# Second biases of a mixture-of-experts layer: added to the routed rows from a fetched table of eight rows, in place of one bias product per output bank

## The chip, the cores and the metric

The kernel runs on one core of a Trainium2 chip. The core has TensorE (PE in the profile), VectorE (DVE), ScalarE (ACT), GpSimd (POOL) and SyncE (SP), each with its own instruction queue that is worked off in order, and 16 DMA engines that all queues share. The metric is the device time of one execution in microseconds, lower is better.

## The reference

Two layers follow each other on x (625 nodes by 1024, f32). The first is a graph layer over 20000 edges of two types. The second, which the change concerns, is a feed-forward layer with two shared experts and eight routed ones, of which each node takes its two best:

```python
sh = _gelu(jnp.einsum('td,sdh->sth', xf, sW1) + sb1[:, None, :])
shared = jnp.einsum('sth,shd->std', sh, sW2) + sb2[:, None, :]
shared = shared.mean(axis=0)
gates = xf @ rW + rb
topk_vals, topk_idx = jax.lax.top_k(gates, TOP_K)
topk_probs = jax.nn.softmax(topk_vals, axis=-1)
...
h = _gelu(jnp.einsum('td,edh->eth', xf, W1) + b1[:, None, :])
y = jnp.einsum('eth,ehd->etd', h, W2) + b2[:, None, :]
moe = jnp.einsum('te,etd->td', w, y)
return (shared + moe).reshape(B, L, D)
```

The second biases are b2 (8 x 1024) and sb2 (2 x 1024). A node's output holds the mean of the two rows of sb2, and the sum of two rows of b2, weighted with its two probabilities, which add up to one.

## The kernel before

The program is one long straight line for the one core. The source calls helpers, and a scheduler places each engine's instructions; within an engine they then run in the order in which they were placed. A call's place in the source therefore doesn't fix where its instructions stand in an engine's queue. `tc.issue_after` holds an instruction back behind another one.

The stages, with the times of the profiled execution:

- Front and counting, to about 100 us. Edges are counted per pair of nodes with one-hot matrices: VectorE builds the one-hots (`ohs`, `ohk`, L849 to L852) and TensorE multiplies them (L868). Between these, node tiles t = 0 to 4 of 125 nodes go through `stats(t)` (VectorE bn_stats L757 and L760, then ScalarE's `h`, L765), `to_columns` (eight TensorE transposes L795; half of the result is written to `nT` by ScalarE, L801, the other half by VectorE, L798), and `project` (L891: eight f32 products over k into one bank, which read both halves of `nT`). The table `at(c, f, ...)` says after which count column each is called; `at(EC - 1, ...)` is the end of the counting. Then come the aggregation (L909) and the activation.
- Output projection of the graph layer and the second layer norm (L952 to L966), 102 to 133 us. GpSimd writes the rows to DRAM as `h2d` and `x1d`.
- Gate, `route`, `slots` and the shared experts' first product (`shared_in`, L1137), 134 to 170 us. `slots` gives each (node, expert) pair a place in NJ = 11 tiles of 128 slots. Two one-hots, `oh` (place in the tile) and `oj` (which tile, times the node's number `tid`), are multiplied (p_tok, L1250), which gives each slot's node. From it come `tok` (row to fetch) and `row` (row to write).
- The routed experts' first product, 170 to 221 us: GpSimd fetches the rows of each tile (`xs`, L1332, an indirect DMA; pool `io` with three buffers), TensorE transposes them (p_x, L1340) and multiplies with W1 (p_h, L1359).
- The routed experts' second product (p_yj, L1417), 221 to 260 us. A tile fills two PSUM banks of 512 columns; they are copied to `ys` by VectorE (L1421, 15 copies) or ScalarE (L1423, 7 copies), and GpSimd writes the tile to DRAM (`yt`, L1425, an indirect DMA).
- The shared experts' second product (p_o, L1472), 260 to 296 us, in eleven banks. SP loads the routed rows of each node from `yt` (`gs`, L1436); VectorE adds them with their weights `wab`, and adds the banks (L1448). The result is stored.

The second biases take this way in the kernel before. At the start GpSimd copies sb2 and b2 into a DRAM tile `bd`, three times over (L625, L627). After `slots`, `bias_parts` loads it (`b2x`) and splits it in three bf16 parts (`b23`); `weights_T` splits the weights `w` (two ones for the shared experts, eight for the routed) likewise and transposes them on TensorE into `wT` (L1298). In the last stage each p_o bank ends with one product of the two:

```python
nc.tensor.matmul(p[:TP, :n], wT[:, own], b23[:, at], start=False, stop=True)   # L1474
```

GpSimd's queue at the start holds, in this order: constants, the loads of `cb`, `vec` and `rb_t`, sums for `join` (L619, L621) with the two `bd` copies among them, and the load of `rw_t`. Its DMAs share eight completion semaphores in turn, so that a DMA waits for the one eight before it. SP's queue holds the loads of x and the weights, the clearing of `yt`, and then the loads of `w1a`, `sw1` and `w2a`.

Of the kernel before, what the change touches and what calls it, by code (L numbers as in the profile page):

```python
# [8 lines left out]
F32 = mybir.dt.float32  # L9
F16 = mybir.dt.float16  # L10
BF16 = mybir.dt.bfloat16
I32 = mybir.dt.int32
# [440 lines left out]
def sparse_kernel(  # L453
# [166 lines left out]
    for i in (2, 3):  # L620
        nc.gpsimd.tensor_add(join, join, ident[:, QC * i : QC * (i + 1)])  # L621


    bd = dram.tile([3, NS + NE, D], F32, name="bd")
    nc.gpsimd.dma_start(bd[:, :NS, :], bass.AP(tensor=sb2.tensor, offset=sb2.offset,  # L625
                                               ap=[[0, 3], [D, NS], [1, D]]))
    nc.gpsimd.dma_start(bd[:, NS:, :], bass.AP(tensor=b2.tensor, offset=b2.offset,  # L627
                                               ap=[[0, 3], [D, NE], [1, D]]))
    b23 = const.tile([3 * QC, D], BF16, name="b23")

    def bias_parts():
        b2x = io.tile([3 * QC, D], F32, tag="io", name="b2x")
        nc.vector.memset(b2x, 0.0)
        for j in range(3):
            nc.gpsimd.dma_start(b2x[j * QC : j * QC + 3 * (NS + NE)], bd.rearrange("i e d -> (i e) d"))
        b2h = rt.tile([3 * QC, D], BF16, name="b2h")
        for j in range(3):
            with tc.issue_after(named.ins):
                nc.vector.tensor_copy(b2h, b2x)
            nc.scalar.copy(b23[j * QC : (j + 1) * QC], b2h[j * QC : (j + 1) * QC])  # L640
            if j < 2:
                nc.vector.tensor_sub(b2x, b2x, b2h)

    rw_t = const.tile([128, KD, QC], F32, name="rw_t")
    nc.vector.memset(rw_t[:, :, NE:], 0.0)
# [338 lines left out]
    def at(c, f, *args):  # L984
        after[c].append((f, args))
# [13 lines left out]

    at(50, clear)  # L1000
    at(30, transpose_vec)
    at(6, scales, 0, 2)
    at(18, scales, 2, 4)
    at(21, scales, 4, NT)
# [90 lines left out]


    w = const.tile([TP, NT, NS + NE], F32, name="w")
    wT = hid.tile([3 * QC, N], BF16, name="wT")
    sel = const.tile([TP, NT, NE], F16, name="sel")
    wide = [TP, NT, NE]  # L1100

    def route():
        full = [TP, NT, NE, NE]
        other = gates[:, :, None, :].to_broadcast(full)
        own = gates[:, :, :, None].to_broadcast(full)
        nc.vector.tensor_scalar(lower, lower, 0.0, None, op0=ALU.is_gt)
        above = rt.tile(full, F32, name="above")
        equal = rt.tile(full, F32, name="equal")
        nc.vector.tensor_tensor(above, other, own, op=ALU.is_gt)
        nc.vector.tensor_tensor(equal, other, own, op=ALU.is_equal)  # L1110
        nc.vector.tensor_mul(equal, equal, lower[:, None, :, :].to_broadcast(full))
        nc.vector.tensor_add(above, above, equal)
        cnt = const.tile(wide, F32, name="cnt")
        nc.vector.tensor_reduce(cnt, above, axis=AX.X, op=ALU.add)
        nc.vector.tensor_scalar(sel, cnt, 1.5, None, op0=ALU.is_lt)
        top = const.tile([TP, NT], F32, name="top")
        nc.vector.tensor_reduce(top, gates, axis=AX.X, op=ALU.max)
        ex = const.tile(wide, F32, name="ex")
        nc.vector.tensor_sub(ex, gates, top[:, :, None].to_broadcast(wide))
        nc.scalar.activation(ex, ex, AF.Exp)  # L1120
        nc.vector.tensor_mul(ex, ex, sel)
        tot = const.tile([TP, NT], F32, name="tot")
        nc.vector.tensor_reduce(tot, ex, axis=AX.X, op=ALU.add)
        inv = const.tile([TP, NT], F32, name="tot_inv")
        nc.vector.reciprocal(inv, tot)
        nc.vector.memset(w[:, :, :NS], 1.0)
        nc.vector.tensor_mul(w[:, :, NS:], ex, inv[:, :, None].to_broadcast(wide))


# [15 lines left out]
    wab = const.tile([TP, 2, NT], F32, name="wab")  # L1145
    tok = const.tile([128, NJ], I32, name="tok")
    row = const.tile([128, NJ], I32, name="row")
    ej = const.tile([1, nt + 4], I32, name="ej")

    def slots():  # L1150
# [63 lines left out]
        nc.vector.tensor_reduce(ab[:, 1], m[:, 1], axis=AX.X, op=ALU.max)  # L1214
        both_ = [TP, 2, NT, NE]
        nc.vector.tensor_tensor(m, m, ab[:, :, :, None].to_broadcast(both_), op=ALU.is_equal)
        nc.vector.tensor_mul(m, m, w[:, None, :, NS:].to_broadcast(both_))
        nc.vector.tensor_reduce(wab, m, axis=AX.X, op=ALU.add)
        nc.vector.tensor_scalar(ab[:, 0], ab[:, 0], 4096.0, None, op0=ALU.add)
# [17 lines left out]
        nc.vector.tensor_copy(pc[:, 1], col)  # L1237
        oh = rt.tile([TP, 2, NT, 128], F16, name="oh")
        oj = const.tile([TP, 2, NT, NJ], F16, name="oj")
        q = ps_mm("p_tok")  # L1240
        for a in range(2):
            nc.vector.tensor_tensor(oh[:, a], it[:, None, :].to_broadcast([TP, NT, 128]),
                                    pc[:, 0, a][:, :, None].to_broadcast([TP, NT, 128]), op=ALU.is_equal)
            nc.vector.tensor_tensor(oj[:, a], it[:, None, :NJ].to_broadcast([TP, NT, NJ]),
                                    pc[:, 1, a][:, :, None].to_broadcast([TP, NT, NJ]), op=ALU.is_equal)
            nc.vector.tensor_mul(oj[:, a], oj[:, a], tid[:, a, :, None].to_broadcast([TP, NT, NJ]))
        shared_in(0, 1)
        for a in range(2):
            for t in range(NT):
                nc.tensor.matmul(q[:, :NJ], oh[:, a, t], oj[:, a, t],  # L1250
                                 start=(a == 0 and t == 0), stop=(a == 1 and t == NT - 1))

        t = rt.tile([128, 2, NJ], F32, name="t")
        nc.vector.tensor_scalar(t[:, 0], q[:, :NJ], float(YB), float(YB), op0=ALU.is_ge, op1=ALU.mult)
        nc.vector.scalar_tensor_tensor(t[:, 1], q[:, :NJ], -1.0, t[:, 0], op0=ALU.add, op1=ALU.subtract)
        named = nc.vector.tensor_scalar(tok, t[:, 1], 0.0, float(N - 1), op0=ALU.max, op1=ALU.min)
        nc.vector.tensor_scalar(t[:, 0], q[:, :NJ], 0.5, 4.0 * YB, op0=ALU.is_lt, op1=ALU.mult)
        nc.vector.tensor_tensor(row, t[:, 0], q[:, :NJ], op=ALU.add)

        for at in (0, NH2):  # L1260
            k = kt[:, 0, at : at + NH2]
# [15 lines left out]
        nc.vector.tensor_scalar(ej, es[:, : nt + 4], float(NE - 1), None, op0=ALU.min)  # L1277
        nc.vector.tensor_copy(flagf[:, 1:2], over[:1, 3:4])
        nc.vector.tensor_tensor(flag, flagf[:, 0:1], flagf[:, 1:2], op=ALU.add)
        return named  # L1280

    def weights_T():
        nc.vector.tensor_scalar(w[:, :, NS:], w[:, :, NS:], float(NS), None, op0=ALU.mult)
        NW_ = NS + NE
        part = rt.tile([TP, NT, 3 * QC], F32, name="part")
        nc.vector.memset(part, 0.0)
        near = const.tile([TP, NT, NW_], BF16, name="near")
        for i in range(3):
            nc.vector.tensor_copy(near, w)
            for j in range(3):  # L1290
                at = j * QC + i * NW_
                nc.vector.tensor_copy(part[:, :, at : at + NW_], near)
            if i < 2:
                nc.vector.tensor_sub(w, w, near)
        for a, b in ((0, 3), (3, NT)):
            p = ps_mm(f"p_wT_{a}")
            for d in range(a, b):
                nc.tensor.transpose(p[: 3 * QC, (d - a) * TP : (d - a + 1) * TP], part[:, d, :],  # L1298
                                    ident[:TP, :TP])
            nc.vector.tensor_copy(wT[:, a * TP : b * TP], p[: 3 * QC, : (b - a) * TP])  # L1300

    gate()
    route()
    named = slots()
    weights_T()
    bias_parts()
    for t in range(HK):
        shared_in(1, t)
    sh_in.close()
# [94 lines left out]
    for j in ORDER:  # L1404
        for a, _, e in parts(j)[1:]:
            for k in range(HK):
                w2m[j, a, k] = gat.tile([128, D], F32, tag="y", name=f"w2m_{j}_{a}_{k}")
                nc.scalar.copy(w2m[j, a, k][:, None, :], w2a[:, bass.ds(e, 1), k, :])
    sent = []
    for n, j in enumerate(ORDER):  # L1410
        y = gat.tile([128, D], F32, tag="y", name=f"ys_{j}")
        for s in range(2):
            at = slice(s * 512, (s + 1) * 512)
            p = ps_acc(f"p_yj_{j}_{s}")
            for k in range(HK):
                for a, b, e in parts(j):
                    made = nc.tensor.matmul(p[a:b], hjT[:, j, k, a:b],  # L1417
                                     w2m[j, a, k][:, at] if a else w2a[:, bass.ds(e, 1), k, at],
                                     start=(k == 0), stop=(k == HK - 1))
            if s or n < 4:  # L1420
                nc.vector.tensor_copy(y[:, at], p)  # L1421
            else:
                nc.scalar.copy(y[:, at], p)  # L1423

        sent.append(nc.gpsimd.indirect_dma_start(  # L1425
            out=yt, out_offset=bass.IndirectOffsetOnAxis(ap=row[:, j : j + 1], axis=0), in_=y, in_offset=None,
            bounds_check=2 * YB - 1, oob_is_err=False))
        for s in sent[:-1]:
            tc.declare_no_dep(sent[-1].ins, s.ins, reason="rows of different slots")

    gs = {}
    for d in range(NT):
# [26 lines left out]
    for d in range(NT):  # L1459
# [4 lines left out]
        for at in ((0, 512), (512, D)) if d < NT - 1 else ((0, 512), (512, 768), (768, D)):  # L1464
# [4 lines left out]
            with tc.issue_after(made.ins):  # L1469
                for i in range(NS):  # L1470
                    for k in range(HK):
                        nc.tensor.matmul(p[:TP, :n], shT[:, i, k, own], sw2[:, i, k, at],  # L1472
                                         start=(i == 0 and k == 0), stop=False)
                nc.tensor.matmul(p[:TP, :n], wT[:, own], b23[:, at], start=False, stop=True)  # L1474
            add(x1[:, d, at], p[:TP, :n], 1.0 / NS, x1[:, d, at])
            if d == NT - 1:
                store(d, at)
# [45 lines left out]
```

## Time and profile before

| | |
|---|---|
| time, median of three runs | 304.47 us (304.38 to 305.63) |
| profiled execution, time | 303.7 us |
| profiled execution, span | 301.4 us |
| PE busy | 290.8 us (96%) |
| VectorE busy | 168.4 us (56%) |
| ScalarE busy | 107.5 us (36%) |
| GpSimd busy | 45.2 us (15%) |
| DMA, mean over the span | 203 GB/s |

The span runs from the first to the last instruction; the profiled execution's own time is 2.3 us more. The page shows each engine's busy share in 40 slices of 7.5 us, the chain of waits that ended last, the groups of instructions by line, and the DMA issues. The timeline gives an engine's instructions in order: start and length in us, and in brackets how long the engine sat idle before one and what ended that.

### The profile page before, as it was taken

How to read it: one execution, taken by the hardware profiler on the slowest of the kernel's cores; microseconds unless marked ns; L12 is line 12 of the kernel's file. 1: busy time of each engine (PE TensorE's matmuls, PEld its weight loads, DVE VectorE, ACT ScalarE, POOL GpSimd, SP SyncE). 2: the span in 40 equal slices, each digit the busy share in tenths (PEclk: the TensorE clock that was granted, in tenths of full speed). 3: DMA queues.
4: the chain of work that ended last, by engine and by line, in shares of the span. 5: the costliest groups of instructions: out<-in, count | busy, mean ns of one | idle time of the engine just before them, and what ended most of it. 6: DMA issues, size and time to landing. Idle time of an engine off the chain costs nothing.

```text
span 301.4 us, 4682 instructions
## 1 busy us (share of the span) xinstructions
PE 290.8 (96%) x1649; PEld 194.9 (65%) x1649; DVE 168.4 (56%) x465; ACT 107.5 (36%) x246; POOL 45.2 (15%) x98
## 2 busy tenths in 40 slices
PE   8799999999999799999999999999999999999993
PEld 6687777787889534376777887887843334444452
DVE  5999999998327668756883122212223211255921
ACT  2455118355334432155123244638359311000000
POOL 9500000000000014240131212210003222200000
PEclk9999999999999999999999999999999999999998
DMA  7999910000009999965999253340057555479442
GB/s 243 304 318 393 421 65 2 0 2 1 0 17 340 348 348 391 400 195 182 348 396 410 86 203 96 114 141 3 0 190 276 221 209 210 191 291 385 161 138 73
DMA packets 27408, 61.15 MB, mean 203 GB/s; under 512 B 2176, under 2 KB 16007, under 8 KB 27375
## 3 DMA queue, kind: packets, MB, share of 16 engines
q1 hardware_dynamic: 21806, 43.77, 40.7%
q0 software_dynamic: 5280, 16.69, 15.7%
q10 hardware_dynamic: 294, 0.35, 0.5%
q8 instruction: 15, 0.25, 0.3%
q14 instruction: 13, 0.10, 0.1%
HBM read 42.76 MB, written 18.81 MB: 204 GB/s over the span
## 4 chain that ended last, share of the span: by engine, by line
PE 93%; DVE 4%; ACT 1%; issue 0%; ACTq 0%
PE p_pr L891 20%; PE p_h L1359 13%; PE p_yj L1417 13%; PE p_o L1472 11%; PE p_sh L1137 10%; PE p_y L952 6%; PE p_agg L909 6%; PE p_x L1340 3%; PE p_t L795 3%; PE cnt L868 2%; PE p_y L956 2%; PE p_hT L1371 1%; PE scrap L972 1%; PE p_gate L1085 1%; PE p_o L1474 1%; DVE ln_4s L727 0%
## 5 line engine op out<-in xcount | busy, mean ns | idle before, releaser
L891 PE MATMUL p_pr<-wg,nT 128*125 128x286 f32 x240 | 62.5, 409 | 0.0
L891 PEld LDWEIGHTS p_pr<-wg,nT 128*125 128x125 f32 x240 | 43.2, 187 | 11.3 <-ACT nT L801 0.2
L1359 PE MATMUL p_h<-w1a,xsT 128*128 (+2 forms) x176 | 40.0, 380 | 0.0
L1417 PE MATMUL p_yj<-w2a,hjT 128*128 (+2 forms) x88 | 38.6, 594 | 0.0
L1472 PE MATMUL p_o<-sw,shT 128*125 128x512 f32 (+1 forms) x88 | 36.1, 553 | 0.0
L1137 PE MATMUL p_sh<-h2T,sw 128*128 128x313 f32 (+1 forms) x128 | 35.2, 428 | 0.0
L1359 PEld LDWEIGHTS p_h<-w1a,xsT 128*128 128x128 f32 (+2 forms) x176 | 28.7, 168 | 7.4 <-issue 0.5
L1137 PEld LDWEIGHTS p_sh<-h2T,sw 128*128 128x128 f32 x128 | 23.6, 189 | 8.6 <-issue 0.2
L1417 PEld LDWEIGHTS p_yj<-w2a,hjT 128*128 128x128 f32 (+2 forms) x88 | 14.4, 168 | 22.4 <-issue 22.4
L1472 PEld LDWEIGHTS p_o<-sw,shT 128*125 128x125 f32 x88 | 16.4, 187 | 16.9 <-issue 16.2
L1421 DVE COPY ys<-p_yj 128x512 f32<-128x512 f32 x15 | 10.4, 692 | 28.7 <-PE p_yj L1417 26.5
L1363 DVE COPY hj<-p_h 128x256 f32<-128x256 f32 x11 | 4.7, 425 | 30.8 <-PE p_h L1359 30.8
L909 PE MATMUL p_agg<-P,CT 125*125 125x287 bf16 x150 | 20.1, 287 | 1.6 <-DVE agg L915 1.6
L966 POOL DMA_DIRECT2D x1d<-xh x10 | 5.3, 532 | 98.5 <-DVE xh L959 98.5
L909 PEld LDWEIGHTS <-CT 125*125 125x125 bf16 x150 | 18.5, 136 | 2.5 <-issue 2.0
L1425 POOL DMA_INDIRECT yt<-ys,row x11 | 10.8, 984 | 50.5 <-DVE ys L1421 50.5
L952 PE MATMUL p_y<-wo_t,eT 128*125 128x512 f32 x40 | 18.1, 595 | 0.0
L1332 POOL DMA_INDIRECT xs<-h2d,tok x11 | 11.2, 1015 | 45.0 <-PE p_x L1340 30.9
L1374 ACT ACTIVATE hjT<-p_hT,vT 128x128 f32<-128x128 f32 (+2 forms) x34 | 8.7, 332 | 24.5 <-PE p_hT L1371 24.5
L1344 DVE COPY xsT<-p_x 128x512 f32<-128x512 f32 x11 | 7.6, 692 | 17.4 <-PE p_x L1340 13.8
L1448 DVE SCALAR_TENSOR_TENSOR x<-p_o,x 125x512 f32<-125x512 f32 (+1 forms) x11 | 6.9, 641 | 16.3 <-PE p_o L1474 16.3
L1359 PE MATMUL p_h<-w1m,xsT 128*64 128x256 f32 (+1 forms) x96 | 14.7, 381 | 0.0
(302 smaller groups left out, 424.0 us busy)
## 6 DMA issues: line engine op xcount, KB each, us to landing
w1a<-in_L_ffn_W_dram SPq DMA_DIRECT2D x8, 1024.0 KB, 10.5
w2a<-in_L_ffn_W_dram SPq DMA_DIRECT2D x8, 1024.0 KB, 4.8
yt<-zero SPq DMA_DIRECT2D x2, 2560.0 KB
g<-yt SPq DMA_DIRECT2D x10, 512.0 KB, 6.7
sw<-in_L_ffn_sW_dram SPq DMA_DIRECT2D x4, 1024.0 KB, 5.0
x<-x1d SPq DMA_DIRECT2D x5, 500.0 KB
wg<-in_L_gnn_W_rel_dram SPq DMA_DIRECT2D x2, 1144.0 KB, 19.1
x1d<-xh POOLq DMA_DIRECT2D x5, 448.0 KB, 6.7
```

The costliest lines, as they stand in the source:

```text
L795: nc.tensor.transpose(pv[:, k, :], row[:, at : at + 128], ident[:TP, :TP])
L891: nc.tensor.matmul(p[:TP, :F], nT[:, k, m * TP : (m + 1) * TP], wg[:, k, r, :], start=(k == 0), stop=(k == KD - 1))
L909: nc.tensor.matmul(p[:TP, : F + 1], CT[:, m, at : at + TP], P[:, m, r, i], start=(m == 0 and i == 0), stop=(m == NT - 1 and i == 2))
L952: nc.tensor.matmul(ps[s][:TP, :], eT[:, k, :], wo_t[:, k, s * 512 : (s + 1) * 512], start=(k == 0), stop=False)
L1137: nc.tensor.matmul(p[:, : z - a], sw1[:, i, k, t * 128 : (t + 1) * 128], h2T[:, k, a:z], start=(k == 0), stop=(k == KD - 1))
L1332: nc.gpsimd.indirect_dma_start(out=xs, out_offset=None, in_=h2d, in_offset=bass.IndirectOffsetOnAxis(ap=tok[:, j : j + 1], axis=0))
L1340: nc.tensor.transpose(p[:, k * 128 : (k + 1) * 128], xs[:, at : at + 128], ident)
L1359: nc.tensor.matmul(p[a:b, :H], xsT[j][:, k, a:b], w1m[j, a][:, 0, k, :] if a else w1a[:, bass.ds(e, 1), k, :], start=(k == 0), stop=(k == ...
L1417: made = nc.tensor.matmul(p[a:b], hjT[:, j, k, a:b], w2m[j, a, k][:, at] if a else w2a[:, bass.ds(e, 1), k, at], start=(k == 0), stop=(k = ...
L1421: nc.vector.tensor_copy(y[:, at], p)
L1425: sent.append(nc.gpsimd.indirect_dma_start(out=yt, out_offset=bass.IndirectOffsetOnAxis(ap=row[:, j : j + 1], axis=0), in_=y, in_offset=No ...
L1472: nc.tensor.matmul(p[:TP, :n], shT[:, i, k, own], sw2[:, i, k, at], start=(i == 0 and k == 0), stop=False)
```

## The change

The biases of the routed rows are added where a tile's PSUM banks are copied out, from a table of eight rows in DRAM (`b2d`). Row e holds b2[e] plus half of each row of sb2; as a node's two weights add up to one, the mean of sb2 comes in whole through its two routed rows. The table is made at the start: three GpSimd DMAs load sb2[0] and sb2[1] (each repeated for the eight experts) and b2 into `b2p` (128 partitions, 64 columns each), `bias_rows` adds them with two VectorE instructions, and SP stores the sum. `slots` gets a second product (p_slot), of `oh` with `oe` (the tile's one-hot times the expert's number), which gives each slot's expert, `es_`. `fetch_bias(j)` fetches a row of the table for each of the tile's 128 slots with an indirect DMA from GpSimd, into the pool `io`; three are issued ahead of the p_yj loop, and one behind each `yt` write after that. The copies to `ys` become VectorE additions, all 22 of them. `bd`, `b2x`, `b23`, `bias_parts`, `weights_T`, `wT` and the eleven bias products go.

```diff
-    bd = dram.tile([3, NS + NE, D], F32, name="bd")
-    nc.gpsimd.dma_start(bd[:, :NS, :], bass.AP(tensor=sb2.tensor, offset=sb2.offset,
-                                               ap=[[0, 3], [D, NS], [1, D]]))
-    nc.gpsimd.dma_start(bd[:, NS:, :], bass.AP(tensor=b2.tensor, offset=b2.offset,
-                                               ap=[[0, 3], [D, NE], [1, D]]))
-    b23 = const.tile([3 * QC, D], BF16, name="b23")
-
-    def bias_parts():
-        b2x = io.tile([3 * QC, D], F32, tag="io", name="b2x")
-        nc.vector.memset(b2x, 0.0)
-        for j in range(3):
-            nc.gpsimd.dma_start(b2x[j * QC : j * QC + 3 * (NS + NE)], bd.rearrange("i e d -> (i e) d"))
-        b2h = rt.tile([3 * QC, D], BF16, name="b2h")
-        for j in range(3):
-            with tc.issue_after(named.ins):
-                nc.vector.tensor_copy(b2h, b2x)
-            nc.scalar.copy(b23[j * QC : (j + 1) * QC], b2h[j * QC : (j + 1) * QC])
-            if j < 2:
-                nc.vector.tensor_sub(b2x, b2x, b2h)
+    b2d = dram.tile([NE, D], F32, name="b2d")
+    BC = 128 // NE
+    b2p = fbig.tile([128, NS + 1, D // BC], F32, name="b2p")
+    for i, v in enumerate((sb2[0], sb2[1], b2)):
+        of = v.offset
+        ap = [[D // BC, 128], [1, D // BC]] if i == NS else [[0, NE], [D // BC, BC], [1, D // BC]]
+        nc.gpsimd.dma_start(b2p[:, i], bass.AP(tensor=v.tensor, offset=of, ap=ap))
+
+    def bias_rows():
+        for i in range(NS):
+            nc.vector.scalar_tensor_tensor(b2p[:, NS], b2p[:, i], 1.0 / NS, b2p[:, NS], op0=ALU.mult, op1=ALU.add)
+        nc.sync.dma_start(b2d.rearrange("e (c w) -> (e c) w", c=BC), b2p[:, NS])
...
+    at(EC - 1, bias_rows)
...
+        expert = const.tile([TP, 2, NT], F16, name="expert")
+        me = const.tile([TP, 2, NT, NE], F16, name="me")
+        nc.vector.tensor_tensor(me.rearrange("p a t e -> p (a t) e"), m.rearrange("p a t e -> p (a t) e"),
+                                it[:, None, :NE].to_broadcast([TP, 2 * NT, NE]), op=ALU.mult)
...
+        with nc.allow_low_precision("whole numbers up to 7"):
+            nc.vector.tensor_reduce(expert, me, axis=AX.X, op=ALU.add)
...
+            nc.vector.tensor_mul(oe[:, a], oj[:, a], expert[:, a, :, None].to_broadcast([TP, NT, NJ]))
             nc.vector.tensor_mul(oj[:, a], oj[:, a], tid[:, a, :, None].to_broadcast([TP, NT, NJ]))
...
+        q2 = ps_mm("p_slot")
+        for a in range(2):
+            for t in range(NT):
+                nc.tensor.matmul(q2[:, :NJ], oh[:, a, t], oe[:, a, t],
+                                 start=(a == 0 and t == 0), stop=(a == 1 and t == NT - 1))
...
+        nc.vector.tensor_scalar(es_, q2[:, :NJ], float(NE - 1), None, op0=ALU.min)
...
-    def weights_T():
-        nc.vector.tensor_scalar(w[:, :, NS:], w[:, :, NS:], float(NS), None, op0=ALU.mult)
...
-        for i in range(3):
-            nc.vector.tensor_copy(near, w)
-            for j in range(3):
-                at = j * QC + i * NW_
-                nc.vector.tensor_copy(part[:, :, at : at + NW_], near)
-            if i < 2:
-                nc.vector.tensor_sub(w, w, near)
-        for a, b in ((0, 3), (3, NT)):
-            p = ps_mm(f"p_wT_{a}")
-            for d in range(a, b):
-                nc.tensor.transpose(p[: 3 * QC, (d - a) * TP : (d - a + 1) * TP], part[:, d, :],
-                                    ident[:TP, :TP])
-            nc.vector.tensor_copy(wT[:, a * TP : b * TP], p[: 3 * QC, : (b - a) * TP])
...
-    sent = []
+    sent, biases = [], {}
+
+    def fetch_bias(j):
+        biases[j] = io.tile([128, D], F32, tag="io", name=f"b2_{j}")
+        nc.gpsimd.indirect_dma_start(out=biases[j], out_offset=None, in_=b2d,
+                                     in_offset=bass.IndirectOffsetOnAxis(ap=es_[:, j : j + 1], axis=0))
+
+    for j in ORDER[:3]:
+        fetch_bias(j)
...
-            if s or n < 4:
-                nc.vector.tensor_copy(y[:, at], p)
-            else:
-                nc.scalar.copy(y[:, at], p)
+            nc.vector.tensor_tensor(y[:, at], p, biases[j][:, at], op=ALU.add)
...
+        if n + 3 < NJ:
+            fetch_bias(ORDER[n + 3])
...
                         nc.tensor.matmul(p[:TP, :n], shT[:, i, k, own], sw2[:, i, k, at],
-                                         start=(i == 0 and k == 0), stop=False)
-                nc.tensor.matmul(p[:TP, :n], wT[:, own], b23[:, at], start=False, stop=True)
+                                         start=(i == 0 and k == 0), stop=(i == NS - 1 and k == HK - 1))
```

More of the change, by code (lines that the diff above doesn't have):

```diff
@@ L1097, in sparse_kernel @@
     w = const.tile([TP, NT, NS + NE], F32, name="w")
-    wT = hid.tile([3 * QC, N], BF16, name="wT")
     sel = const.tile([TP, NT, NE], F16, name="sel")
@@ L1125, in route @@
         nc.vector.reciprocal(inv, tot)
-        nc.vector.memset(w[:, :, :NS], 1.0)
         nc.vector.tensor_mul(w[:, :, NS:], ex, inv[:, :, None].to_broadcast(wide))
@@ L1147, in sparse_kernel @@
     row = const.tile([128, NJ], I32, name="row")
+    es_ = const.tile([128, NJ], I32, name="es_")
     ej = const.tile([1, nt + 4], I32, name="ej")
@@ L1239, in slots @@
         oj = const.tile([TP, 2, NT, NJ], F16, name="oj")
+        oe = const.tile([TP, 2, NT, NJ], F16, name="oe")
+        with nc.allow_low_precision("whole numbers up to 7"):
+            nc.vector.tensor_reduce(expert, me, axis=AX.X, op=ALU.add)
         q = ps_mm("p_tok")
@@ L1255, in slots @@
         nc.vector.scalar_tensor_tensor(t[:, 1], q[:, :NJ], -1.0, t[:, 0], op0=ALU.add, op1=ALU.subtract)
-        named = nc.vector.tensor_scalar(tok, t[:, 1], 0.0, float(N - 1), op0=ALU.max, op1=ALU.min)
+        nc.vector.tensor_scalar(tok, t[:, 1], 0.0, float(N - 1), op0=ALU.max, op1=ALU.min)
         nc.vector.tensor_scalar(t[:, 0], q[:, :NJ], 0.5, 4.0 * YB, op0=ALU.is_lt, op1=ALU.mult)
         nc.vector.tensor_tensor(row, t[:, 0], q[:, :NJ], op=ALU.add)
+        nc.vector.tensor_scalar(es_, q2[:, :NJ], float(NE - 1), None, op0=ALU.min)
         for at in (0, NH2):
@@ L1279, in slots @@
         nc.vector.tensor_tensor(flag, flagf[:, 0:1], flagf[:, 1:2], op=ALU.add)
-        return named
-    def weights_T():
-        nc.vector.tensor_scalar(w[:, :, NS:], w[:, :, NS:], float(NS), None, op0=ALU.mult)
[L1284 to L1287, printed above, removed]
-        for i in range(3):
-            nc.vector.tensor_copy(near, w)
-            for j in range(3):
-                at = j * QC + i * NW_
-                nc.vector.tensor_copy(part[:, :, at : at + NW_], near)
-            if i < 2:
-                nc.vector.tensor_sub(w, w, near)
-        for a, b in ((0, 3), (3, NT)):
-            p = ps_mm(f"p_wT_{a}")
-            for d in range(a, b):
-                nc.tensor.transpose(p[: 3 * QC, (d - a) * TP : (d - a + 1) * TP], part[:, d, :],
-                                    ident[:TP, :TP])
-            nc.vector.tensor_copy(wT[:, a * TP : b * TP], p[: 3 * QC, : (b - a) * TP])
     gate()
     route()
-    named = slots()
-    weights_T()
-    bias_parts()
+    slots()
     for t in range(HK):
```

## The prediction

> **What bounds the kernel now.** I read first the busy tenths of the page, then the chain that ended last in order of time, then the engine timelines around the places the change touches.
>
> ```profile
> PE   8799999999999799999999999999999999999993
> ...
> DVE  5999999998327668756883122212223211255921
> ...
> DMA  7999910000009999965999253340057555479442
> ...
> PE 93%; DVE 4%; ACT 1%; issue 0%; ACTq 0%
> ```
>
> Each digit covers 7.5 us. TensorE (PE) is full from the third slice to the last but one, and the chain is 93% PE. So every PE instruction added or removed counts at its full length, and whatever makes PE wait counts too. In slices 1 to 8 VectorE (DVE) is as full as PE: there it has no time in hand either. The DMA engines are full in slices 1 to 4, when x and the weights come in.
>
> The chain in the front stage (start, length, what):
>
> ```profile
> 10.30 0.29 PE cnt L868 x4
> 10.62 1.07 PE p_t L795 x8
> 11.70 0.11 PE cnt L868 x4
> 11.81 4.10 PE p_pr L891 x16
> 15.91 0.06 PE cnt L868 x2
> ```
>
> These are the first count matmuls, the transposes of node tile 0, and its first projection: eight f32 products over k (16 records, since each has two), of which the last four (from 11.81 + 2.05 = 13.86) read the half of nT that VectorE writes in to_columns. VectorE's timeline at that place (start, length, instruction, idle before it):
>
> ```profile
> 10.69 0.47 DVE L850 TENSOR_TENSOR ohs<-ohs,cols 125x512 f16<-125x512 f16 x1
> 11.74 0.68 DVE L798 TENSOR_TENSOR nT<-p_t,lT 128x500 f32<-128x500 f32 x1 [0.57 <-PE p_t L795]
> 12.33 1.28 DVE L757 BATCH_NORM_STATS2 st<-xh 125x6 f32<-125x512 f32 x2
> ```
>
> VectorE is free at 10.69 + 0.47 = 11.16; the eviction ends at 12.42, 1.44 before PE needs it. GpSimd's (POOL's) timeline shows when it issues the bias rows:
>
> ```profile
> 10.51 0.55 POOL L625 DMA_DIRECT2D bd<-in_L_ffn_sb_dram  x1 [2.34 <-DMA cb<-in_L_gnn_conv_bias_dram]
> 11.08 0.27 POOL L621 TENSOR_TENSOR join<-join,ident 128x32 f32<-128x32 f32 x1
> 11.28 0.53 POOL L627 DMA_DIRECT2D bd<-in_L_ffn_b_dram  x1
> 11.82 0.26 POOL L621 TENSOR_TENSOR join<-join,ident 128x32 f32<-128x32 f32 x1
> 12.02 0.96 POOL L646 DMA_DIRECT2D rw_t<-in_L_ffn_rW_dram  x1
> ```
>
> and the DMA list how long such transfers take from issue to landing (last column):
>
> ```profile
> bd<-in_L_ffn_b_dram POOLq DMA_DIRECT2D x1, 96.0 KB, 7.3
> ...
> rw_t<-in_L_ffn_rW_dram POOLq DMA_DIRECT2D x1, 32.0 KB, 7.7
> ...
> bd<-in_L_ffn_sb_dram POOLq DMA_DIRECT2D x1, 24.0 KB, 7.9
> ```
>
> Nobody on the path waits for bd before 143 us, so today these landings cost nothing.
>
> **What the Trainium skill says.** "DMA: Bandwidth & Descriptors", section "Anatomy of one DMA — SWDGE (gpsimd) path", prices a GpSimd DMA at about 2.0 us plus bytes over 436e3 per us; for 32 KB that would be an estimated 2.1 us. The trace disagrees: 6.1 to 7.9 us in this stretch, where the DMA engines are full. I use the trace. "TensorE: Matmul & The Clock Gate", section "Part 1: The HAM clock gate", says that after an idle window of about 3.4 us TensorE runs at half clock until it has been busy about as long. The trace agrees on the warming: the first 24 scrap matmuls take 2.74 us (114 ns each), the later 40 take 2.41 us (60 ns each). It has no idle gap long enough to show the cooling; the longest there is 1.69 us. "Perfetto Trace Analysis", section "Per-engine timelines", puts the wait for a semaphore in a queue ahead of execution; GpSimd shows the effect here: its join sum at 11.08 needs no DMA, yet stands behind the 2.34 us wait for cb.
>
> **The change part by part.**
>
> 1. *Bias products gone.* In the chain the eleven products at L1474 are nine of 0.22 and two of 0.11 and 0.13: 2.2 us off PE in the last stage, all on the path.
>
> 2. *weights_T and bias_parts gone.* The five transposes L1298 stand in the chain with 0.54 us: off. Their VectorE work (memset, three casts, two subtractions of 96x1024) and three ScalarE copies of 1.04 us lie beside p_sh, with PE busy throughout: nothing. GpSimd is freed of the 4.3 us it waited behind them; its gathers start earlier, but PE takes up the first p_x at 170.21 without a gap today: nothing.
>
> 3. *Expert per slot.* Ten p_slot matmuls like the ten of p_tok (0.24 us): +0.24. Four small VectorE instructions (me, its reduction, two oe) come ahead of the last oj, in steps of about 0.12 us: 0.5. The last oj ends at 152.28, PE arrives at 152.49, so PE waits about 0.3. Together +0.5 (bounds 0.2 to 0.8).
>
> 4. *The table.* b2p is filled by three GpSimd DMAs where bd had two, and bias_rows folds the shared biases in with two VectorE instructions of 128x64. The source calls bias_rows at the end of the counting, but the order of instructions as the changed kernel is built puts the two at rows 34 and 35 of VectorE, straight behind the ohs product that ends at 11.16 and ahead of the nT eviction; the first waits for the first and third b2p DMA. GpSimd's order: the first b2p still waits for cb (10.51), the second takes 11.28, the third stands where rw_t was, 12.02 to 12.5 (128 rows may take 0.8 to issue, as cb's 125 did). With 7.5 us to landing, between bd's and rw_t's: 12.1 + 7.5 = 19.6. VectorE stands from 11.16 to 19.6; two instructions of some 0.2 us follow; the eviction starts at 20.0 in place of 11.74: **VectorE is 8.3 us late**. Behind it in its queue are the statistics of tile 1, the one-hots of the next groups, and so everything PE gets. PE stops at 13.86 and resumes at 20.7: 6.8 late. It then catches nothing up, and loses more in two ways: half clock for about the 2.7 to 4.7 us that warming took at the start (from PE's first work at 1.5 or 2.5 to 5.2 or 6.2), costing half of that, 1.4 to 2.3; or, without it, ScalarE's h of tile 3, which follows VectorE's neg at 22.30 and ends at 23.72 for a p_t at 23.81, so that VectorE's 8.3 come through less 0.1. These overlap, they don't add: 8.2 on one path, 6.8 + 1.9 = 8.7 on the other. I take **8.6**. Later nothing absorbs it, as PE has no idle time until 96 us and little after. Bounds: landing after 6.1 (the shortest of this stretch) takes 1.5 off; 8 us and a slow issue add 1.
>
> 5. *b2d's store.* One 32 KB DMA on SP, between the two yt clears and the w1a loads. It waits for VectorE's two instructions, long done by then, and the w1a loads behind it wait for work up to 88 us: nothing.
>
> 6. *The gathers.* Eleven indirect DMAs on GpSimd, by the nearest row (xs: 0.94 to 1.4 us to issue, 4.4 to landing), three ahead, then one behind each scatter. GpSimd idles 2.4 us or more before each scatter, so 0.94 fits. The first three need io buffers freed by the last p_x groups (204 to 214), well before 222. A later gather is issued about 2 us after a tile ends and used 8.6 us after: 4.4 fits. They add 5.8 MB to the 40 us of p_yj; the DMA share there is 0.61, and 5.8 MB at about 385 GB/s (the 235 GB/s of that stretch over its 0.61) is 15 us of 39, or 0.38. That fills the engines but for bursts. I take nothing, bounds 0 to 4.
>
> 7. *The adds.* 22 VectorE additions from PSUM in place of 15 copies there and 7 on ScalarE: like L959 (125x512, 0.67 against the copy's 0.69), 15 us in a stage of 38: nothing.
>
> Sum: -2.2 - 0.5 + 0.5 + 8.6 = **+6.4**. The profiled execution had a span of 301.4 and took 303.7 us, 0.8 under the median 304.47; so 310.1 for such an execution, and 310.9 against the median.
>
> **The rivals.**
>
> *No stall: faster.* The place is the same two instructions; the price is only the landing. If it came by 11.5 us nothing would wait and -2.2 us would be left: 302.3. VectorE's lateness breaks even at 2.3 us, a landing at about 13.6, or 1.5 us after issue; above that the kernel is slower. Against it stand all landings of GpSimd's DMAs in this stretch, 6.1 or more. For it, only that SBUF rows of 256 bytes land sooner than bd did in DRAM; rw_t went to SBUF and took 7.7. Chance 0.06, with 0.02 for a landing that just balances.
>
> *A shorter stall.* Landing 4.4 after issue, as xs later: VectorE 5.2 late, PE 5.1, net +3: 307.5. Chance 0.07.
>
> *The gathers collide with the scatters.* All rows of a tile are mostly the same 4 KB of DRAM, and gathers share GpSimd's queue with the scatters. If scatters end so late that the g loads slip by more than 4 us past 268, PE and the last adds wait: another 4, 315. Against it: cb is one row read 125 times and landed in 6.7, like rows read once. Chance 0.07.
>
> **How the numbers follow.** The forecast has 0.78, at 310.9; its bounds (landing, clock, step 3) give 308.0 to 312.8. Adding the shorter stall's near edge, I give 307.8 to 312.8, which leaves out the no-stall and collision rivals. Half a per cent, 1.5 us, is about what a measurement can tell from no change. Faster 0.06, same 0.02, slower 0.92.
>
> **What would show it.** In the changed profile: the b2p instructions on VectorE with about 8 us of idle before them on a DMA; PE idle about 7 us in slice 1 or 2, then p_pr products longer for some 4 us; all later stages late by about 8.6, the p_o stage 2.2 shorter; y additions with no wait on a bias. A b2p wait under 3 us proves step 4 wrong; p_yj with gaps, or g loads that end later against p_o, prove step 6 wrong.

## The result, and the profile after

The changed kernel takes 318.13 us (median of six runs, 316.82 to 319.91), the kernel before 305.08 us in the same session. The ratio is 1.0436, with a 95% interval of 1.0407 to 1.0465: slower by 4.4%. The forecast was slower, 310.9 us, with a range of 307.8 to 312.8. The direction came out; the forecast added 6.4 us to the median of 304.47 that it started from, about half of the 13 us measured, and the time lies above the range.

The profiled execution has a span of 315.8 us, 14.4 more than before. Its page shows two holes in PE's row, one in slices 2 and 3 and one in slices 33 to 35 (a slice is 7.9 us here; the row PEclk is the granted TensorE clock, in tenths of full speed):

```profile
PE   8629999999999899999999999999999986799993
...
PEclk9969999999999999999999999999999999999999
```

The first hole is the forecast one. GpSimd's timeline, then VectorE's, then PE's, at the place shown for the kernel before:

```profile
10.72 0.67 POOL L630 DMA_DIRECT2D b2p<-in_L_ffn_sb_dram  x1 [2.58 <-DMA cb<-in_L_gnn_conv_bias_dram]
...
12.44 0.62 POOL L630 DMA_DIRECT2D b2p<-in_L_ffn_b_dram  x1
```

```profile
10.69 0.42 DVE L843 TENSOR_TENSOR ohs<-ohs,cols 125x512 f16<-125x512 f16 x1
20.48 0.48 DVE L634 SCALAR_TENSOR_TENSOR b2p<-b2p 128x64 f32<-128x64 f32 x2 [9.38 <-DMA b2p<-in_L_ffn_b_dram]
20.88 0.67 DVE L791 TENSOR_TENSOR nT<-p_t,lT 128x500 f32<-128x500 f32 x1
```

```profile
11.79 2.19 PE L884 MATMUL p_pr<-wg,nT 128*125 128x286 f32 x8
21.61 3.79 PE L884 MATMUL p_pr<-wg,nT 128*125 128x286 f32 x8 [7.63 <-DVE nT L791]
```

VectorE stands idle for 9.4 us, until the last b2p transfer has landed; the nT eviction comes at 20.88 in place of 11.74, and PE is idle for 7.6 us. The next eight records take 3.79 us, where the eight before the stall took 2.19: the granted clock was half of full speed from 18.05 to 24.9 us, and the clock row has its 6 there.

The second hole was not forecast. The groups that waited most (engine, line, what it waited for: us, times, longest), and the DMA list with the median to landing last:

```profile
DVE ys L1412 <- DMA b<-b2d,es__1591: 24.2, 7, 5.2
...
PE p_yj L1409 <- DVE ys L1412: 5.8, 4, 1.7
```

```profile
b<-b2d,es__1591 POOLq DMA_INDIRECT x11, 12.1
yt<-ys,row POOLq DMA_INDIRECT x11, 10.7
```

The bias rows land 12.1 us after their issue in the median (the profile gives a landing for six of the eleven gathers: the first took 4.5 us, the others 7.4 to 13.8). VectorE waits for them, the PSUM banks stay full meanwhile, and PE waits for banks. VectorE's timeline shows the pace that results, one tile about every 5.2 us where PE alone needs 3.4 (the step between the tiles before the first of these waits):

```profile
247.22 1.29 DVE L1412 TENSOR_TENSOR ys<-p_yj,b 128x512 f32<-128x512 f32 x2 [5.19 <-DMA b<-b2d,es__1591]
252.37 1.29 DVE L1412 TENSOR_TENSOR ys<-p_yj,b 128x512 f32<-128x512 f32 x2 [3.86 <-DMA b<-b2d,es__1591]
257.60 1.29 DVE L1412 TENSOR_TENSOR ys<-p_yj,b 128x512 f32<-128x512 f32 x2 [3.94 <-DMA b<-b2d,es__1591]
```

The balance follows from the starts of PE's groups in the two traces. At the last run of p_agg before the activation PE is late by 9.5 us (98.10 against 88.62), at the first p_x by 9.6 (179.62 against 170.04), at the first p_yj still by 9.6 (230.6 against 221.0), at the first p_o by 16.4 (275.9 against 259.5), at the end of the last addition by 14.2 (310.89 against 296.68). So the front cost 9.5, `slots` and the first products 0.1, **the second-product stage (first p_yj to first p_o) 6.8** (45.3 us against 38.5), and the p_o stage gave 2.2 back.

### The profile page after: what moved, and what is told of

Same layout as the page of the kernel before. It is cut to its first block, busy times and chain, and to the rows that moved or that the text cites. A ratio compares the mean times of both kernels' runs of the same rounds, so it can differ in the third digit from the quotient of the medians.

```text
span 315.8 us, 4651 instructions
## 1 busy us (share of the span) xinstructions
PE 292.1 (92%) x1643; PEld 194.8 (62%) x1643; DVE 165.4 (52%) x454; ACT 100.2 (32%) x236; POOL 54.6 (17%) x107
## 4 chain that ended last, share of the span: by engine, by line
PE 51%; issue 22%; DMA 11%; POOL 8%; DVE 6%; ACT 0%; POOLq 0%; DVEq 0%; ACTq 0%
PE p_pr L884 19%; PE p_o L1463 11%; PE p_y L945 5%; PE p_agg L902 5%; DMA b<-b2d,es__1591 4%; DMA xs<-h2d,tok 3%; DMA b2p<-in_L_ffn_b_dram 3%; POOL b L1397 2%; POOL xs L1316 2%; DMA cb<-in_L_gnn_conv_bias_dram 2%; PE p_t L788 2%; POOL yt L1414 2%; PE p_sh L1129 2%; PE p_y L949 2%; PE cnt L861 2%
## 5 line engine op out<-in xcount | busy, mean ns | idle before, releaser
L884 PE MATMUL p_pr<-wg,nT 128*125 128x286 f32 x240 | 64.3, 418 | 7.6 <-DVE nT L791 7.6
L884 PEld LDWEIGHTS p_pr<-wg,nT 128*125 128x125 f32 x240 | 44.2, 191 | 19.9 <-DVE nT L791 8.1
L1409 PE MATMUL p_yj<-w2a,hjT 128*128 (+2 forms) x88 | 39.7, 599 | 5.8 <-DVE ys L1412 5.8
L1463 PE MATMUL p_o<-sw,shT 128*125 128x512 f32 (+1 forms) x88 | 34.5, 553 | 0.0
L1412 DVE TENSOR_TENSOR ys<-p_yj,b 128x512 f32<-128x512 f32 x22 | 14.5, 688 | 35.0 <-DMA b<-b2d,es__1591 24.2
L1316 POOL DMA_INDIRECT xs<-h2d,tok x11 | 10.4, 950 | 55.3 <-PE p_x L1324 34.9
L1439 DVE SCALAR_TENSOR_TENSOR x<-g,wab,x 125x1024 f32<-125x1024 f32 x10 | 12.6, 1283 | 4.7 <-DMA g<-yt 4.5
```

What stands on the lines that cost most here:

```text
L884: nc.tensor.matmul(p[:TP, :F], nT[:, k, m * TP : (m + 1) * TP], wg[:, k, r, :], start=(k == 0), stop=(k == KD - 1))
L1316: nc.gpsimd.indirect_dma_start(out=xs, out_offset=None, in_=h2d, in_offset=bass.IndirectOffsetOnAxis(ap=tok[:, j : j + 1], axis=0))
L1409: made = nc.tensor.matmul(p[a:b], hjT[:, j, k, a:b], w2m[j, a, k][:, at] if a else w2a[:, bass.ds(e, 1), k, at], start=(k == 0), stop=(k = ...
L1412: nc.vector.tensor_tensor(y[:, at], p, biases[j][:, at], op=ALU.add)
L1439: added.append(nc.vector.scalar_tensor_tensor(*args, op0=ALU.mult, op1=ALU.add))
```

## The experiments

The first hole was put down to one wait, and that had to be tested. For the second hole there were three theories. A: the loads of x1, which SP issues at the start of the stage, occupy five of the 16 DMA engines, and the gathers and scatters have to pass through these five as well as the others. B: all 128 descriptors of a tile read the same one or few 4 KB rows of the table, and that is slow. C: GpSimd's queue cannot carry a gather behind every scatter.

A comes from what the Trainium skill says in "DMA: Bandwidth & Descriptors", section "Why a DMA increments its semaphore by 16 and not by 1": a transfer is spread over the largest number of engines, at most 16, that divides the outermost dimension of both its sides. An x1 load has 125 rows, so five. The DMA rows of the changed kernel, 40 slices of 245 to 270 us, agree:

```profile
DMA  9999633369889833496799333984977336578963
GB/s 380 374 380 334 210 144 131 131 249 380 282 282 367 302 118 131 184 406 243 216 419 295 131 125 131 367 341 184 380 282 288 144 125 262 203 197 347 328 203 118
```

Again and again the share falls to three tenths at about 131 GB/s. Five of 16 engines are 0.31, and 131 over five is 26 GB/s each, as much as each has when all are busy (420 over 16).

**late_rows**: the table's two VectorE instructions are held behind the last one-hot (`hot` collects the `ohk` instructions).

```diff
+    hot = []
+
     def bias_rows():
         for i in range(NS):
+          with tc.issue_after(hot[-1].ins):
             nc.vector.scalar_tensor_tensor(b2p[:, NS], b2p[:, i], 1.0 / NS, b2p[:, NS], op0=ALU.mult, op1=ALU.add)
...
-            nc.vector.tensor_tensor(halves(oh_k[:, :g, :]), row[:, None, :SPAN].to_broadcast(shape), key,
-                                    op=ALU.is_equal)
+            hot.append(nc.vector.tensor_tensor(halves(oh_k[:, :g, :]), row[:, None, :SPAN].to_broadcast(shape), key,
+                                               op=ALU.is_equal))
```

> The changed kernel, with the two bias_rows instructions held behind VectorE's last one-hot; nothing else changes. If the early wait for b2p costs what the profile of the changed kernel shows at the front (PE 9.5 us later at 98 us than before), 318.1 - 9.5 = 308.6 us, the second-product stage still 44 us long. If the front delay is taken up somewhere later, less than 5 us come back.

Measured: 309.87 us, ratio 1.016 (1.0125 to 1.0195), 8.3 us less than the changed kernel, 1.2 short of what was expected. In its chain the group of p_agg is back at its old start, and p_o starts late all the same:

```profile
88.62 7.47 PE p_agg L905 x60
...
266.27 34.37 PE p_o L1466 x88
```

The second-product stage runs from 221.1 to 266.1, 45.0 us. So the whole front delay seen in the profile came from that one wait, nothing took it up later, and the second hole stands by itself.

**x1_wide**: each x1 load in two parts, of 112 rows, which 16 divides, and 13 (`PARTS` are rows 0 to 111 and 112 to 124).

```diff
-        nc.sync.dma_start(x1[:, t, :], x1d[t * TP : (t + 1) * TP, :])
+        for g in PARTS:
+            nc.sync.dma_start(x1[g, t, :], x1d[t * TP + g.start : t * TP + g.stop, :])
```

> The changed kernel, with each x1 load of 125 rows issued as two (112 and 13 rows); nothing else changes. Theory A (five of the 16 DMA engines carry the x1 loads and are shared with gathers and scatters; they set the pace of 5.2 us a tile): the second-product stage falls from 44 to about 37.5 us, gathers land in about 5 us, 318.1 - 7 = 311 us. Theory B (a tile's 128 descriptors read one 4 KB row of DRAM, and that is slow) and theory C (GpSimd's queue is too slow for a gather behind each scatter): no change, 318.

Measured: 311.88 us, ratio 1.0241 (1.0196 to 1.0286), 6.3 us less. The stage runs from 231.1 to 270.7, 39.6 us. The DMA rows in 40 slices of 245 to 266 us no longer fall to three tenths:

```profile
DMA  9999999999999999999999889739899994967667
GB/s 273 281 289 273 281 304 304 359 421 445 382 281 242 289 343 429 429 398 437 414 406 445 359 336 421 312 133 343 242 250 297 414 336 187 304 195 203 242 258 320
```

GpSimd's queue moved 5.83 MB in these 21 us (278 GB/s), against 4.64 MB in 25 us (186 GB/s) of the changed kernel. The same gathers read the same rows through the same queue, so B and C cannot be what held them. The stage is still 1.1 us longer than the 38.5 before, and 2 us longer than expected: the engines are now full (a mean share of 0.94 over the stage), and while the x1 loads run one gather still takes 13.5 us, for which PE waits 0.9 us:

```profile
240.66 13.51 DMA b<-b2d,es__1591
```

**rows_apart**: as many gathers of the same size, but from rows that differ. The rows added are then not the biases, so that this run is for its time alone.

```diff
-        nc.gpsimd.indirect_dma_start(out=biases[j], out_offset=None, in_=b2d,
-                                     in_offset=bass.IndirectOffsetOnAxis(ap=es_[:, j : j + 1], axis=0))
+        nc.gpsimd.indirect_dma_start(out=biases[j], out_offset=None, in_=h2d,
+                                     in_offset=bass.IndirectOffsetOnAxis(ap=tok[:, j : j + 1], axis=0))
```

> The changed kernel, but each bias gather reads the rows of h2d named by tok (128 different rows over 2.5 MB of DRAM) in place of the rows of b2d, so that the added rows are not the biases; the number and size of all DMAs stay. Theory B (one hot row is slow): gathers land in 4 to 6 us, the second-product stage is about 37.5 us, 311 us. Theories A and C: gathers still land in about 12 us, 318.

Measured in two executions: 318.59 us, ratio 1.0445 (1.0399 to 1.0491), stage 231.5 to 276.3 (44.8 us). B falls: nothing changes when the rows lie apart. The gather that PE waits for last takes as long as before; the changed kernel's line is first, this run's second:

```profile
260.48 12.75 DMA b<-b2d,es__1591
...
260.98 12.68 DMA b<-h2d,tok
```

The median to landing in this run is 7.6 us and not 12, which the expectation had wrong. But late_rows, which gathers from `b2d`, has 7.7 with a stage as long as here, so this median over the few landings that are known does not tell the kernels apart.

**x1_narrow**: two DMAs per x1 load as in x1_wide (the edit is shown against it), but of 115 and 10 rows, so that by the rule above the large one stays on five engines.

```diff
-        for g in PARTS:
+        for g in (slice(0, 115), slice(115, TP)):
```

> The changed kernel, with each x1 load issued as two DMAs, as in x1_wide, but of 115 and 10 rows: 115 divides by 5 and by no larger number up to 16, so that it stays on five DMA engines. Theory A (five engines are shared): second-product stage again 44 to 45 us, about 317 to 318 us. If smaller or more DMAs alone helped in x1_wide, about 39.5 us and 312.

Measured: 317.74 us, ratio 1.0397 (1.0348 to 1.0446). The stage takes 45.5 us, and its p_o starts where the changed kernel's (276.08) does. Its DMA rows of 245 to 270 us fall to three tenths at 131 GB/s again:

```profile
276.13 34.37 PE p_o L1464 x88
...
DMA  9999433349879943398789533698899546478953
GB/s 374 321 400 275 164 131 131 131 164 387 334 249 347 374 131 131 131 387 315 203 367 321 171 118 131 269 374 269 242 315 334 157 157 197 197 203 354 367 171 131
```

So it is the spread over engines that counted in x1_wide, not the split in two.

**both**: late_rows and x1_wide together.

> The changed kernel with both edits: bias_rows held behind the last one-hot, x1 loads in two parts. If both theories hold, nothing is left of the change but what it saves on PE, 2.2 us of bias products and about 0 in slots: 305.1 - 2.2 = 302.9 us, faster than before by 0.7%. If theory B or C holds in place of A, 308.6.

Measured: 302.43 us, ratio 0.9922 (0.9901 to 0.9944): faster than the kernel before by 0.8%, and 15.7 us faster than the change as made. This version beats both kernels. PE has one gap left in the second-product stage, 0.7 us, and the stage takes 39.4 us (222.1 to 261.5) where the kernel before has 38.5:

```profile
245.81 0.62 PE L1413 MATMUL p_yj<-w2a,hjT 128*32 x1 [0.70 <-DVE ys L1416]
```

The gain is read from the medians. The profiled execution took 303.1 us, 0.7 more than the median, and its front is 1.0 us late (its group of p_agg starts at 89.62, where late_rows, with the same front, has 88.62); its last addition ends only 0.2 us before that of the kernel before (296.48 against 296.68).

**before_x1_wide**: the kernel before, with the x1 loads of x1_wide and nothing else.

> The kernel before, with the x1 loads in two parts of 112 and 13 rows; nothing else changes. Its second-product stage is bound by PE (no PE idle time in it), so the time should stay at 305 us within half a per cent, while the scatters land sooner than their 7.3 us, in about 4. If x1_wide gains in itself, 302 to 303.

Measured: 306.59 us, ratio 1.0053 (1.0037 to 1.0068). The wide loads gain nothing in the kernel before, so the gain of `both` is not one that they would bring without the change. The scatters do land sooner, with a median of 3.3 us in place of 7.3 (the line gives minimum, median and maximum):

```profile
DMA to landing us min/median/max: 3.2/3.3/9.8
```

PE's stage is 38.5 us as before and the last addition 0.2 us later. The rest of its longer span (303.7 against 301.4) lies behind the last addition, where SP waits for PE's queue at the program's end. What causes that was not looked into; that the interval reaches 0.7% was not expected.

**warm**: scrap matmuls that keep PE busy while VectorE waits.

```diff
+    def keep_warm(n):
+        p = ps_acc("scrap2")
+        for _ in range(n):
+            nc.tensor.matmul(p[:, :128], iota, iota, start=True, stop=True)
...
         at(c1, to_columns, t, None, nT, True)
+        if t == 0:
+            at(c1, keep_warm, 120)
```

> The changed kernel, with 120 scrap matmuls (about 6.7 us) on PE ahead of the first count product, so that PE stands idle for less than 3 us while VectorE waits for b2p. VectorE's wait stays. If the idle time cools PE's clock, the eight records of the first projection behind the stall take 2.1 us in place of 3.8, and PE is about 8 us late at 98 us in place of 9.5: 316.5. If the slow records had another cause, 318 and 3.8 us.

Measured: 326.50 us, ratio 1.0674 (1.064 to 1.0709), 8.4 us *more* than the changed kernel. As a shortening it failed, since the extra matmuls also changed the order in which the scheduler placed the other engines' work: ScalarE writes tile 1's half of nT only behind the h of tile 3, at 31.80, and PE stands again. The records still answer the question, in the timeline of PE and in the clock row of this run's page (slices of 8.1 us):

```profile
21.40 2.19 PE L884 MATMUL p_pr<-wg,nT 128*125 128x286 f32 x8 [2.32 <-DVE nT L791]
...
27.92 0.21 PE L861 MATMUL cnt<-ohk,ohs 125*128 125x58 f16 x1 [2.47 <-DVE ohk L845]
32.20 6.58 PE L884 MATMUL p_pr<-wg,nT 128*125 128x286 f32 x16 [4.08 <-ACT nT L794]
...
PEclk9996799999999999999999999999999999999999
```

With PE kept busy until 19.1 us, the granted clock is still full after 2.3 us of idle, and the eight records take 2.19 us, as if nothing had been; in the changed kernel, at the same time and with the DMA engines as full, they took 3.79. Later sixteen take 6.58, where they take 4.12 at full clock. So the slow records come from a clock that falls when PE does too little. The length of one gap does not tell when it falls: in this run it was at half from 27.0 to 37.2 us, so it fell 1.5 us after PE's last work (25.45), within the gap of 2.5 us and before the one of 4.1.

## Why the prediction was wrong, point by point

- **The step that failed is step 6, the gathers.** It added 0.38 of the DMA engines' time to the 0.61 in use and booked nothing, with bounds of 0 to 4. The measured cost is 6.8 us. The sum of the shares was about right: with the x1 loads spread evenly, the stage runs at a share of 0.94 and costs 1.1 us more than before (x1_wide, 39.6 us). What step 6 had wrong is that it read a mean over 16 engines as if each had that share. The load was not even, and that is the other 5.7 us (45.3 against 39.6).
- How five engines can set the pace, as an estimate: they still had 1.68 MB of the x1 loads to carry in the 25 us from 245 on, 13 KB per us and engine, half of their 26. A tile sends each engine eight gathered rows and some seven scattered ones (1250 rows in eleven tiles), about 61 KB; at the other half's 13 KB per us that is 4.7 us per tile, near the 5.2 seen.
- The sign stood in the profile before. Its DMA rows of 238 to 260 us, which the prediction does not use, fall to three tenths at 127 to 134 GB/s too, and its scatters took 7.3 us to land where they take 3.3 with wide loads (before_x1_wide):

```profile
DMA  9833334973333986233474332389742369831129
GB/s 395 357 142 127 134 127 171 410 306 142 127 134 127 372 335 261 119 141 127 171 283 179 127 134 104 142 350 402 276 179 119 134 261 425 358 134 74 67 112 410
```

- The step also set a landing of 4.4 us against an allowance of 6.6. With up to 13.8 that allowance was gone, so the cover that it named did not hold.
- The rival of colliding gathers had the right place but the wrong mechanism (hot rows, and g loads that slip). The stage itself stretched, with gaps in p_yj, which is the sign that the prediction had named against step 6; the price of 4 was too low and the chance of 0.07 too small.
- **Step 4, the early wait, held in mechanism and nearly in size**: 8.6 forecast, 9.5 measured at the end of the counting. The third b2p DMA was issued at 12.44 and not 12.1, since each b2p took 0.6 to 0.7 us to issue, and its 7.9 to landing was above the 7.5 taken. The eviction came 9.1 us late (8.3 forecast), PE resumed 7.8 late (6.8), and the cool clock cost 1.7 (1.9).
- Step 1 (-2.2) is as measured. Steps 2 and 3 came to +0.1 together, near the forecast 0. PE waited 0.25 us for oj, 0.3 had been taken. Step 5 and step 7 cost nothing: the additions last 0.69, like the copies.
- Sum of the parts measured: 9.5 + 0.1 + 6.8 - 2.2 = 14.2 at the last addition, against the forecast's 6.4; the difference of 7.8 is 6.8 in step 6, 0.9 in step 4 and 0.1 in steps 2 and 3.

The range was too narrow at its upper end for that reason: the collision was left outside it as a rival, although 0.61 and 0.38 in step 6 add up to 0.99, which says that the engines had nothing in hand.

## What to carry to other kernels

Ask how a DMA share is spread over the engines, as the mean hides it: here loads of 125 rows ran on five of 16 engines, stretches at three tenths with 131 GB/s were how that looked, and the gathers and scatters, which needed all 16, moved at the pace of those five. Parts of 112 and 13 rows ended it. Ask where a scheduler put a small instruction that waits for a DMA, as its place in the source doesn't tell; two 0.2 us instructions cost 9.5 us in the profile here for having been placed in front of the work of a full engine. A change can be right (302.4 us with both flaws mended, 0.8% faster) and still measure 4.4% slower.

## What the runs showed of the hardware that was not expected

- Reading one row many times by an indirect DMA cost nothing visible: the first bias gather, with the DMA engines otherwise idle, took 4.5 us to landing for 128 slots that read the eight-row table, and 4.2 in rows_apart for as many rows lying apart.
- GpSimd DMAs of 32 KB took 7.4 to 7.9 us to landing while the loads at the start kept the DMA engines full.
- TensorE's granted clock fell to half 4.1 us after PE had stopped in the changed kernel (13.98 to 18.05), but 2.3 us after in x1_wide, with the same stall (13.98 to 16.25), and 1.5 us after in warm. It then stayed low for 6.8 us in the changed kernel and 10.2 in x1_wide and in warm, so that the eight records behind the stall took 3.79 us in the one and 4.18 in the next. The Trainium skill ("TensorE: Matmul & The Clock Gate", section "What's actually happening") has the clock set by how busy PE was in windows of about 3.4 us that run on whatever the kernel does; 6.8 and 10.2 are two and three of these. Its table has the fall come after an idle window, and there these runs differ: in the 3.4 us before the fall PE still worked 1.2 us in x1_wide and 1.5 in warm.
